# A softmax sum's reciprocal moved from VectorE to ScalarE, and an image's first values loaded by fewer transfers

## Chip, cores and metric

The kernel runs on one core of one Trainium2 chip. The metric is the device time of one execution in microseconds (us); three runs of the kernel before the change give a median of 4012.74 us (4012.72 to 4017.47). Below, PE is TensorE, PEld its weight loads, DVE VectorE, ACT ScalarE, POOL GpSimd, SP the engine whose queue issues nearly all transfers. Each engine works through its own instructions in the program's order and meets the others only at semaphores.

## What is computed

Two residual layers on eight images of 256 channels and 64 x 64 positions, in float32. Cut to what matters:

```
# layer 0: x = x + involution(groupnorm(x))  (1x1 convolutions, a 3x3 weight per position)
# layer 1, on x = groupnorm(x):
q, k, v = 1x1 convolutions of x                     # 4 heads of 64 channels
uk, uv  = 7x7 windows of k + position, v (reflect padding)
out_att = softmax(q . uk) . uv
wts = softmax over 9 taps of (Wfc x)                # 9 weights for each channel and position
oc  = depthwise3x3(relu(depthwise3x3(x, w1)), w2)
out_conv = sum over the 9 taps of oc * wts
x = x + rate1 * out_att + rate2 * out_conv
```

In `out_conv` the same `oc` stands under all nine weights. The kernel takes exponentials relative to one of the taps, sums the other eight (`tot`), adds 1, and multiplies `oc` by the quotient of the sum and itself.

## The kernel before

An image is cut into 8 bands of 8 rows (`R = 8`, `NB = 8`). The program first does layer 0 alone for 12 bands (the loop's `g` from -12 to -1), and then, for 64 bands, layer 1 of band `g` beside layer 0 of a band 10 to 12 places ahead; for the last ten bands no layer 0 is left. Each band of layer 1 has eight steps `s`: two halves of the channels (`ct`), each with four pairs of 8-column tiles (`m`). The order is written out by hand (`manual_schedule`): a step has six places, between which `advance()` is called; work goes in directly, through the lists `mid` and `end` of `beside()`, or by `after(n, f)`, which emits `f` at the n-th `advance()` from there. What is emitted earlier stands earlier in its engine's queue.

In a step, PE does the scores (`sco`, L737), the weighted values (`small <- pt, vt`, L786), two products with `wfc` for the nine weights (`pf`, L873), a transposition (`ptp`, L774), and one or two others: queries, keys (`pk`), values (`pv`, L592), layer 0's maps (L369) and tap weights (`pw`, L466). Most write PSUM tiles of one tag, `gen`, of which there are four; a new one waits until the fourth before it has been read. ACT takes the exponentials of `pf` (`ex`, L878) and of the scores (L759), divides the latter by their sum (L768), and copies. DVE does the depthwise taps (`acc`, L830 and L856), layer 0's products (`prod`, L479), the masked maximum of the scores (`nmax`, L751), a small reciprocal (L766), and the keys with their reflected columns (`kb`, L701 and L708), which the next scores need. POOL adds layer 0's products (`xg`, L487) and the exponentials (`ex`, L1080), copies old keys (L668), and finishes the sum.

`dynamic_sum` (L880 to L911) is emitted four places after the last step of each `ct`, so its parts fall into the steps of the next half band. POOL adds the two halves (L886) and one (L889); 9 and 13 places later DVE takes the reciprocal of half of `tot` each (`quotient`, L894) into `rec`, of which there is one buffer, and POOL multiplies (L895); after 15 places POOL weighs `oc` and adds it to the result `xr` (`weigh`, L899, L900). For `ct = 0` the two reciprocals fall into steps 5 and 6 of the same band, for `ct = 1` into steps 1 and 2 of the next. Only for the very last half band DVE does POOL's part.

Values go through DRAM. `values` makes two halves of a band's `pv` and copies them to `vc` (one buffer); `store_values` writes them to a DRAM tile `vd` with reflected columns; `value_tile` reads `vd` into SBUF tiles `vt` (11 buffers), four for a band (`u`), each for two column groups. At an image's first and last band (`j == 0`, `j == NB`) the reflected rows are read by transfers of their own: eight for a tile in place of two. All of these are issued by SP, in order. An image's first two bands of values are made during the last band of the image before (`made = [(b + 1, 0, 4), (b + 1, 1, 6)]`, the last number being the step); `value_tile` for `j == 0` comes at the end of step 7, for `j == 1` in steps 0, 1 and 2 of the new image's first band, whose step 2 is the first to need them.

Of the kernel before, what the change touches and what calls it, by code (L numbers as in the profile page):

```python
# [12 lines left out]
AF = mybir.ActivationFunctionType  # L13
ALU = mybir.AluOpType
# [9 lines left out]
R = 8  # L24
BAND = R * W
NB = H // R
# [21 lines left out]
PAD = KA // 2  # L48
WP = W + 2 * PAD
TQ = 8  # L50
# [3 lines left out]
KW = TQ + 2 * PAD  # L54
NKEY = KW * KW
CHUNK = R * KW
NPROB = 2 * CHUNK
NEG = -1.0e30


AHEAD = NB + 4
# [25 lines left out]
def conv_layers_kernel(ctx: ExitStack, tc: tile.TileContext, ins: dict, out: bass.AP):  # L87
    nc = tc.nc
# [54 lines left out]
    def rstd_(out_, var, eps):  # L143
        nc.vector.tensor_scalar(out_, var, eps, None, ALU.add)
        nc.scalar.activation(out_, out_, AF.Sqrt)
        nc.vector.reciprocal(out_, out_)


# [61 lines left out]
    images = [Image() for b in range(B)]  # L210
# [4 lines left out]
    def after(n, f):  # L215
        later.append((place[0] + n, f))
# [8 lines left out]
    def gn_affine(sts, means, name, done):  # L225


        n = len(sts)
        mv = stat.tile([P, n, 2], F32, name=f"mv_{name}", tag=f"mv{n}")
        for ct, st in enumerate(sts):  # L230
            nc.vector.bn_aggr(mv[:, ct, :], st)
        mean, var = mv[:, :, 0], mv[:, :, 1]
        gm, d, sc, bi = (stat.tile([P, n], F32, name=f"{v}_{name}", tag=f"{v}{n}") for v in ("gm", "d", "sc", "bi"))

        def group_means(v, k):
            pg = ps.tile([P, n], F32, name=f"pg_{name}_{k}", tag="gen", bufs=4)
            nc.tensor.matmul(pg, means, v, start=True, stop=True)
            return pg


        def a1():
            pg = group_means(mean, 0)
            after(2, lambda: a2(pg))

        def a2(pg):
            nc.vector.tensor_copy(gm, pg)
            for ct in range(n):
                c = slice(ct, ct + 1)
                nc.vector.tensor_scalar(d[:, c], pg[:, c], mean[:, c], None, ALU.subtract)
                nc.vector.tensor_scalar(d[:, c], d[:, c], d[:, c], var[:, c], ALU.mult, ALU.add)  # L250
            after(5, a3)

        def a3():
            pg = group_means(d, 1)
            after(2, lambda: a4(pg))

        def a4(pg):
            nc.vector.tensor_scalar(sc, pg, GN_EPS, None, ALU.add)
            after(2, a5)

        def a5():
            nc.scalar.activation(sc, sc, AF.Sqrt)
            after(4, a6)

        def a6():
            nc.vector.reciprocal(sc, sc)
            for ct in range(n):
                c = slice(ct, ct + 1)
                nc.vector.tensor_scalar(bi[:, c], gm[:, c], sc[:, c], -1.0, ALU.mult, ALU.mult)
            done(sc, bi)  # L270

        after(3, a1)
# [334 lines left out]
    def store_values(b, j):  # L607
# [9 lines left out]
        for d in range(1, PAD + 1):  # L617
            for to, c in ((PAD - d, d), (PAD + W - 1 + d, W - 1 - d)):
# [3 lines left out]
                else:  # L622
                    for p in range(2):
                        o = vd[at + p : at + p + 2 * count[p] - 1 : 2, to : to + 1].rearrange("u c n -> c u n")
                        nc.sync.dma_start(out=o, in_=vc[p * W + c : p * W + c + 1, : count[p]])

    def value_tile(b, j, u):


        im = images[b]  # L630
        vd = im.vd[j]
        vt = im.vt[j, u] = w1.tile([CHUNK, 2, C], F32, tag="vt", name=f"vt_{b}_{j}_{u}", bufs=11)
        if j == 0:
            runs = [(PAD, PAD, R - PAD)] + [(PAD - d, PAD + d, 1) for d in range(1, PAD + 1)]
        elif j < NB:
            runs = [(0, 0, R)]
        else:
            runs = [(0, 1, PAD)] + [(PAD - 1 + d, PAD - d, 1) for d in range(1, PAD + 1)]
        for to, at, n in runs:
            for g in range(2):  # L640
                c0 = (2 * u + g) * TQ
                nc.sync.dma_start(
                    out=vt[to * KW : (to + n) * KW, g], in_=vd[at : at + n, c0 : c0 + KW]
                )

    def new_keys(i):

# [232 lines left out]
    def dynamic_sum(b, i, ct, ex, oc):  # L880

        tot = w1.tile([P, BAND], F32, tag="tots", name=f"tot_{b}_{i}_{ct}", bufs=1)
        xr = images[b].xr[i]

        engine = nc.vector if (b, i, ct) == (B - 1, NB - 1, NCT - 1) else nc.gpsimd
        engine.tensor_add(tot, ex[:, 1], ex[:, 0])  # L886


        engine.tensor_scalar(tot, tot, 1.0, 1.0e37, ALU.add, ALU.min)  # L889
        rec = w1.tile([P, BAND // 2], F32, tag="rec", name=f"rec_{b}_{i}_{ct}", bufs=1)  # L890

        def quotient(u):
            v = tot[:, u * BAND // 2 : (u + 1) * BAND // 2]
            nc.vector.reciprocal(rec, v)  # L894
            after(1, lambda: engine.tensor_mul(v, v, rec))  # L895

        def weigh():

            engine.tensor_mul(oc, oc, tot)  # L899
            engine.tensor_add(xr[:, ct], xr[:, ct], oc)  # L900
            if ct == NCT - 1:
                after(6, store)

        def store():
            nc.sync.dma_start(
                out=out[b].rearrange("(t p) n -> p t n", p=P)[:, :, i * BAND : (i + 1) * BAND], in_=xr
            )

        after(9, lambda: quotient(0))
        after(13, lambda: quotient(1))  # L910
        after(15, weigh)  # L911


    def beside(g, s):

        b, i = divmod(g, NB)
        bn, inx = divmod(g + 1, NB)
        mid, end = [], []

        early = i in (0, NB - 1)  # L920
        if g >= 0:
            if s == 2 - early:
                mid.append(lambda: queries(b, i, 1))
            if s == 3 - early:
                mid.append(lambda: keys(b, i, 1))
        early = inx in (0, NB - 1)
        if 0 <= g + 1 < B * NB:
            if s == 5 - early:
                mid.append(lambda: position(bn, inx))
            if s == 6 - early:  # L930
                mid.append(lambda: queries(bn, inx, 0))
            if s == 7 - early:
                mid.append(lambda: keys(bn, inx, 0))

        made = [(b, i + 2, 4)] if g >= 0 and i < NB - 1 else []
        if i == NB - 1 and 0 <= b + 1 < B:
            made = [(b + 1, 0, 4), (b + 1, 1, 6)]
        for bb, j, d in made:
            if s in (d, d + 1) and (j < NB or s == d):
                mid.append(lambda bb=bb, j=j, d=d: values(bb, j, s - d))  # L940
            if s == d + 1:
                end.append(lambda bb=bb, j=j: store_values(bb, j))
            if s == 7 and d == 4:
                for u in range(NT // 2):
                    end.append(lambda bb=bb, j=j, u=u: value_tile(bb, j, u))
        if g >= 0 and i == 0 and s in (0, 1, 2):
            for u in {0: (0,), 1: (1,), 2: (2, 3)}[s]:
                end.append(lambda u=u: value_tile(b, 1, u))

        nxt = [(b, i + 2, 0)] if g >= 0 and i + 2 < NB else []  # L950
        if i == NB - 1 and 0 <= b + 1 < B:
            nxt = [(b + 1, 0, 0), (b + 1, 1, 1)]
        for bb, ii, d in nxt:
            if s == d:
                end.append(lambda bb=bb, ii=ii: load_rows(bb, ii))
            if s in (d + 1, d + 2):
                end.append(lambda bb=bb, ii=ii, d=d: normalise(bb, ii, s - d - 1))

        alone = g < 0
        if 0 <= g + AHEAD < B * NB:  # L960
            bq_, iq = divmod(g + AHEAD, NB)
            if alone and s == 0:
                mid.append(lambda: small_maps(bq_, iq, small_tile(f"{bq_}_{iq}"))())
            if s == (2 if alone else 0):
                (mid if alone else end).append(lambda: value_maps(bq_, iq, 0))
            if s == (3 if alone else 1):
                mid.append(lambda: value_maps(bq_, iq, 1))
        if 0 <= g + AHEAD - 1 < B * NB and s == (2 if alone else 1):
            bh, ih = divmod(g + AHEAD - 1, NB)

            def hidden():
                parts = hidden_maps(bh, ih, alone)
                if not alone:
                    convs.extend(parts)

            end.append(hidden)
        if 0 <= g + AHEAD - 2 < B * NB and s in TAPS_AT[g < -1]:
            u = TAPS_AT[g < -1].index(s)
            end.append(
                lambda: tap_weights(*divmod(g + AHEAD - 2, NB), u, g < -1, PRODUCTS_AT[g < -1][u])  # L980
            )
        return mid, end
# [24 lines left out]
    with tc.manual_schedule():  # L1007
# [21 lines left out]
        for g in range(-AHEAD, B * NB):  # L1029
            b, i = divmod(g, NB)  # L1030
            for s in range(STEPS):
                ct, m = divmod(s, NT // 2)
                mid, end = beside(g, s)
                steer(g, s)
                if g >= 0:
# [17 lines left out]
                    tot = exponentials(nm, prob, nmax)  # L1053
# [23 lines left out]
                if g >= 0:  # L1077
# [6 lines left out]
                    if m == NT // 2 - 1:  # L1084
                        oc = depthwise_end(b, i, ct, conv[1])
# [96 lines left out]
```

## Time and profile before

| what | value |
|---|---|
| runs | 4012.74 us median of 3 |
| the profiled execution | 4010.67 us; span 4008.9 us from first to last instruction, granted clock 0.988 |
| PE, DVE, ACT, POOL busy | 3807.0, 3419.8, 2839.5, 3174.8 us |
| layer 0 alone, up to the first scores | 246.3 us |
| DVE reciprocals of the sum (L894) | 256 of 1742 ns, 445.9 us |
| POOL products with them (L895) | 254 of 730 ns, 185.4 us |
| transfers `vt <- vd` issued by SP | 960 |

Busy time is the time in which an engine has an instruction running; matmuls are pipelined, so a PE shown busy can still be short of its peak. A wait is idle time of an engine just before an instruction, put down to the instruction that released it. Timeline rows begin with the start in us from the span's start and the duration; neighbouring equal instructions are merged (x2, x3).

### The profile page before, as it was taken

What the parts mean: (1) busy time and instruction counts of PE and PEld (TensorE: products, weight loads), DVE (VectorE), ACT (ScalarE), POOL (GpSimd) and SP (SyncE); (2) the same over time, 40 slices, a digit from 0 to 9 for tenths busy, and PEclk for the clock granted to TensorE, in tenths of its full rate; (3) what the DMA queues carried; (4) which work ended last, traced back from release to release, by engine and by line L of the source; (5) the groups of instructions that cost most, each with busy time, mean ns of one, the idle gap of its engine ahead of it and who ended that gap; (6) DMA issues with size and microseconds to landing.
All of it is one profiled execution on the core that took longest, in us unless ns stands there. A gap on an engine that the chain in (4) does not pass through costs nothing.

```text
span 4008.9 us, 72420 instructions
## 1 busy us (share of the span) xinstructions
PE 3807.0 (95%) x24620; PEld 2116.9 (53%) x24620; DVE 3419.8 (85%) x7143; ACT 2839.5 (71%) x6779; POOL 3174.8 (79%) x2156
## 2 busy tenths in 40 slices
PE   6879999999999999999999999999999999999998
PEld 3445555555555555555555555555555555555554
DVE  5868988888888988888988888978988889977888
ACT  3457777677676777777777677777777677676776
POOL 4758988788987988878887888978888888965665
PEclk9989999999999999999999999999999999999999
DMA  8864543544444443444443544444443544322220
GB/s 230 201 165 113 134 114 104 136 125 113 127 115 122 124 124 101 125 132 120 124 115 104 138 125 118 110 130 124 118 115 90 129 116 104 85 61 88 71 65 32
DMA packets 493171, 469.42 MB, mean 117 GB/s; under 512 B 68432, under 2 KB 394624, under 8 KB 492544
## 3 DMA queue, kind: packets, MB, share of 16 engines
q1 hardware_dynamic: 489472, 460.23, 43.4%
q10 hardware_dynamic: 3328, 4.55, 0.3%
q8 instruction: 195, 3.19, 0.3%
q14 instruction: 176, 1.44, 0.1%
HBM read 325.64 MB, written 138.99 MB: 116 GB/s over the span
## 4 chain that ended last, share of the span: by engine, by line
PE 27%; POOL 26%; DVE 22%; ACT 10%; issue 7%; DMA 5%; SPq 3%; POOLq 0%; DVEq 0%; ACTq 0%
PE pf L873 13%; POOL xg L487 13%; POOL ex L1080 6%; DVE prod L479 5%; DVE acc L856 5%; DVE rec L894 4%; PE small L786 3%; ACT x L343 3%; PE sco L737 2%; PE ptp L774 2%; ACT ex L878 2%; DVE prob L751 2%; DMA x3q<-x 2%; PE pq L672 2%; DVE acc L830 2%
## 5 line engine op out<-in xcount | busy, mean ns | idle before, releaser
L873 PE MATMUL pf<-yp,c_wfc 128*128 128x512 f32 x4096 | 1917.1, 597 | 6.2 <-ACT ex L878 5.1
L487 POOL TENSOR_TENSOR xg<-xg,prod 128x1024 f32<-128x1024 f32 x549 | 1200.7, 2187 | 177.2 <-DVE prod L479 148.3
L873 PEld LDWEIGHTS pf<-yp,c_wfc 128*128 128x128 f32 x4096 | 744.0, 191 | 730.3 <-issue 647.1
L1080 POOL TENSOR_TENSOR ex<-ex,ex 128x1024 f32<-128x1024 f32 x384 | 907.9, 2364 | 55.9 <-ACT ex L878 51.8
L479 DVE SCALAR_TENSOR_TENSOR prod<-pw,c_par,x3q 128x1040 f32<-128x1040 f32 x576 | 737.9, 1288 | 124.8 <-PE pw L466 56.1
L830 DVE SCALAR_TENSOR_TENSOR acc<-yp,c_chan,acc 128x504 f32<-128x504 f32 (+3 forms) x1104 | 775.0, 702 | 50.7 <-ACT acc L821 30.3
L856 DVE SCALAR_TENSOR_TENSOR acc<-hid,c_chan,acc 128x504 f32<-128x504 f32 (+3 forms) x1024 | 749.8, 732 | 18.1
L878 ACT ACTIVATE ex<-pf 128x512 f32<-128x512 f32 x1024 | 602.1, 588 | 204.2 <-PE pf L873 184.3
L759 ACT ACTIVATE prob<-prob,nmax 128x196 f32<-128x196 f32 x1024 | 459.2, 451 | 217.1 <-DVE nmax L751 216.9
L768 ACT ACTIVATE prob<-prob,tot 128x196 f32<-128x196 f32 x1024 | 413.0, 452 | 235.3 <-DVE tot L766 235.1
L895 POOL TENSOR_TENSOR tot<-tot,rec 128x256 f32<-128x256 f32 x254 | 185.4, 730 | 412.9 <-DVE rec L894 387.9
L894 DVE RECIPROCAL rec<-tot 128x256 f32<-128x256 f32 x256 | 445.9, 1742 | 17.2 <-POOL tot L889 12.3
L776 ACT COPY pt<-ptp 112x512 f32<-112x512 f32 x511 | 294.8, 577 | 123.4 <-PE ptp L774 122.3
L751 DVE CUSTOM_DVE_ANT_0 prob<-sco,c_mask 128x196 f32<-128x196 f32 x1024 | 324.5, 354 | 20.4 <-PE sco L737 20.2
L786 PE MATMUL small<-pt,vt 112*64 112x64 f32 x8144 | 300.3, 226 | 37.5 <-DMA vt<-vd 37.1
L774 PEld LDWEIGHTS ptp<-ident,prob 128*112 128x112 f32 x2044 | 228.1, 134 | 188.9 <-issue 135.2
L774 PE MATMUL ptp<-ident,prob 128*112 128x128 f32 x2044 | 322.9, 281 | 1.3 <-ACT vc L600 1.3
L786 PEld LDWEIGHTS small<-pt,vt 112*64 112x64 f32 x8144 | 261.5, 138 | 116.7 <-issue 75.4
L737 PE MATMUL sco<-kb,qb 64*64 64x196 f32 x4096 | 236.1, 343 | 39.6 <-DVE kb L708 32.9
L592 PE MATMUL pv<-c_wv,yp 128*128 128x256 f32 (+1 forms) x1056 | 252.8, 382 | 2.6 <-ACT ex L878 2.1
L369 PE MATMUL p<-xc,w3s 128*128 128x512 f32 x512 | 248.4, 609 | 7.0 <-ACT ex L878 7.0
L466 PEld LDWEIGHTS pw<-h2n,c_c 128*128 128x128 f32 x1152 | 173.3, 191 | 153.5 <-issue 113.1
(139 smaller groups left out, 4756.9 us busy)
## 6 DMA issues: line engine op xcount, KB each, us to landing
vt<-vd SPq DMA_DIRECT2D x448, 112.0 KB
x<-x3n SPq DMA_DIRECT2D x128, 264.0 KB
x3q<-x SPq DMA_DIRECT2D x128, 264.0 KB
xc<-in_x SPq DMA_DIRECT2D x64, 512.0 KB
xg<-in_x SPq DMA_DIRECT2D x256, 128.0 KB
x<-xg SPq DMA_DIRECT2D x256, 128.0 KB
yp<-x SPq DMA_DIRECT2D x128, 256.0 KB
xr<-x SPq DMA_DIRECT2D x64, 512.0 KB
```

The lines of the kernel that those rows point to most:

```text
L479: nc.vector.scalar_tensor_tensor(prod[:, :, :RUN], pw[:, j, :RUN].unsqueeze(1).to_broadcast([P, SHARE, RUN]), par[:, PCB2 + k : PCB2 + k + 1],
L487: nc.gpsimd.tensor_add(im.xg[i], im.xg[i], rows(prod))
L759: nc.scalar.activation(prob[:, h, :NKEY], prob[:, h, :NKEY], AF.Exp, bias=nmax[:, h : h + 1], scale=-1.0, accum_out=tot[:, h : h + 1],)
L768: nc.scalar.activation(prob[:, h, :NKEY], prob[:, h, :NKEY], AF.Copy, scale=tot[:, h : h + 1])
L774: nc.tensor.transpose(ptp[:, h, ch], prob[:, h, ch * CHUNK : (ch + 1) * CHUNK], ident)
L786: nc.tensor.matmul(po[half[h], :, t * TQ : (t + 1) * TQ], im.vt[i + ch, m][:n, t, (2 * ct + h) * HD : (2 * ct + h + 1) * HD], pt[:n, h, ch ...
L830: nc.vector.scalar_tensor_tensor(o, yp[:, ct, ra + dr : rb + dr, ca + dc : cb + dc], chan[:, ct, CW1 + k : CW1 + k + 1], o, ALU.mult, ALU.add,
L856: nc.vector.scalar_tensor_tensor(o, hid[:, ra + dr : rb + dr, ca + dc : cb + dc], chan[:, ct, CW2 + k : CW2 + k + 1], o, ALU.mult, ALU.add,)
L873: nc.tensor.matmul(pf, wfc[:, kt, 2 * m + j, ct * P : (ct + 1) * P], images[b].yp[i][:, kt, PAD : PAD + R], start=(kt == 0), stop=(kt == N ...
L878: nc.scalar.activation(ex[:, j].rearrange("p (r c) -> p r c", r=R), pf, AF.Exp)
L894: nc.vector.reciprocal(rec, v)
L1080: after(4, lambda ex=ex, exb=exb: nc.gpsimd.tensor_add(ex, ex, exb))
```

## The change

It has three parts. The sum's reciprocal: the two DVE reciprocals and two POOL products of a half band become, for each half of `tot`, a logarithm and an exponential of its negative on ACT (into `rec`), and two places later a Newton step of two DVE instructions, which turn `v = tot` into `tot * rec` and then into `(v - 2) * v`, that is the negative of the quotient; `weigh` therefore subtracts, and comes at place 17 instead of 15. The upper bound of the sum is lowered so that its logarithm stays in range, and the ACT table set that holds both functions is loaded by name after each square root. An image's first values: they are made one step sooner, and `value_tile` for its second band is emitted in the middle of steps 0 and 2. Reflected rows: `mirror_rows` copies three rows inside `vd`, DRAM to DRAM, two steps after the values' second step, so that `value_tile` reads a tile with two transfers everywhere.

```diff
+SUM_MAX = 9.0e18
+TABLES = "natural_log_exp_and_others"
...
         nc.scalar.activation(out_, out_, AF.Sqrt)
+        nc.scalar.preload_act_table_set(TABLES)
...
             nc.scalar.activation(sc, sc, AF.Sqrt)
+            nc.scalar.preload_act_table_set(TABLES)
...
+    def mirror_rows(b, j):
+        vd = images[b].vd[j]
+        for d in range(1, PAD + 1):
+            to, at = (PAD - d, PAD + d) if j == 0 else (PAD + d, PAD - d)
+            nc.sync.dma_start(out=vd[to], in_=vd[at])
...
-        if j == 0:
-            runs = [(PAD, PAD, R - PAD)] + [(PAD - d, PAD + d, 1) for d in range(1, PAD + 1)]
-        elif j < NB:
-            runs = [(0, 0, R)]
-        else:
-            runs = [(0, 1, PAD)] + [(PAD - 1 + d, PAD - d, 1) for d in range(1, PAD + 1)]
-        for to, at, n in runs:
-            for g in range(2):
-                c0 = (2 * u + g) * TQ
-                nc.sync.dma_start(
-                    out=vt[to * KW : (to + n) * KW, g], in_=vd[at : at + n, c0 : c0 + KW]
-                )
+        at, n = (0, R) if j < NB else (1, 2 * PAD)
+        for g in range(2):
+            c0 = (2 * u + g) * TQ
+            nc.sync.dma_start(out=vt[: n * KW, g], in_=vd[at : at + n, c0 : c0 + KW])
...
-        engine.tensor_scalar(tot, tot, 1.0, 1.0e37, ALU.add, ALU.min)
+        engine.tensor_scalar(tot, tot, 1.0, SUM_MAX, ALU.add, ALU.min)
...
-            nc.vector.reciprocal(rec, v)
-            after(1, lambda: engine.tensor_mul(v, v, rec))
+            nc.scalar.activation(rec, v, AF.Ln)
+            nc.scalar.activation(rec, rec, AF.Exp, scale=-1.0)
+            after(2, lambda: refine(v))
+
+        def refine(v):
+            nc.vector.scalar_tensor_tensor(v, v, 1.0, rec, ALU.mult, ALU.mult)
+            nc.vector.scalar_tensor_tensor(v, v, 2.0, v, ALU.subtract, ALU.mult)
...
-            engine.tensor_add(xr[:, ct], xr[:, ct], oc)
+            engine.tensor_sub(xr[:, ct], xr[:, ct], oc)
...
-        after(15, weigh)
+        after(17, weigh)
...
-            made = [(b + 1, 0, 4), (b + 1, 1, 6)]
+            made = [(b + 1, 0, 3), (b + 1, 1, 5)]
...
+            if s == d + 2 and j in (0, NB):
+                end.append(lambda bb=bb, j=j: mirror_rows(bb, j))
-            if s == 7 and d == 4:
+            if s == 7 and j != 1:
...
-        if g >= 0 and i == 0 and s in (0, 1, 2):
-            for u in {0: (0,), 1: (1,), 2: (2, 3)}[s]:
-                end.append(lambda u=u: value_tile(b, 1, u))
+        if g >= 0 and i == 0 and s in (0, 2):
+            for u in (s, s + 1):
+                mid.append(lambda u=u: value_tile(b, 1, u))
```

## The prediction

> **What bounds the kernel now.** I read the busy table first, then busy time by stretches, then the waits, and last the timeline of one ordinary band. In the stretches below the columns are span, busy time of PE, PEld, DVE, ACT and POOL (with instruction counts), clock, DMA share and GB/s; the second is most of one band (it runs from 2003.00 to 2061.70), the third lies in the last image, where layer 0 has ended.
>
> ```profile
> PE 3807.0 (95%) x24620; PEld 2116.9 (53%) x24620; DVE 3419.8 (85%) x7143; ACT 2839.5 (71%) x6779; POOL 3174.8 (79%) x2156
> ```
> ```profile
> 2015.50:2061.50 46.00, 44.98 (x295) 25.43 (x294) 43.62 (x86) 32.79 (x78) 41.40 (x27) 1.00 0.47 118
> ```
> ```profile
> 3800.00:3900.00 100.00, 100.00 (x643) 54.50 (x642) 80.06 (x186) 72.73 (x180) 61.64 (x43) 1.00 0.23 70
> ```
>
> PE sets the pace: without layer 0 it never idles. With it, PE loses little, but DVE is busy 43.62 of 46 us and POOL 41.40 (90%): DVE runs level with PE from step 1 to the band's end, and what it gains or loses there soon reaches PE. PE's own waits (total us, times, longest):
>
> ```profile
> PE small L786 <- DMA vt<-vd: 37.1, 15, 8.0
> ...
> PE sco L737 <- DVE kb L708: 32.9, 58, 1.3
> ```
>
> The first is an image's first band waiting for values; the second is the scores of steps 0 and 4 waiting for DVE's keys. Nothing else is as large, so a gain is worth some 70 us at most, plus a little.
>
> **The values.** At an image's start SP issues 32 small `vt` transfers before it gets to the second band's:
>
> ```profile
> 1695.41 16.97 SPq L642 DMA_DIRECT2D vt<-vd  x32
> ...
> 1718.38 1.42 SPq L642 DMA_DIRECT2D vt<-vd  x2
> ```
>
> With two for a tile it is 8 of 16.97/32 = 0.53 us, 4.2 us; 24 go, 12.7 us, and three row copies (estimated at the same 0.5 us each on SP) go in two steps earlier. The second band's store now stands ahead of them, and its first four loads follow, so they land some 10 us sooner, against a longest wait of 8.0: -37.1 us, bounds -37.1 and 0. The same number of transfers goes for each image's last band. Against this: the values' copies into the single `vc` wait for the store of the first band, 14 issues in 1682.36 to 1691.9. Now the second copy follows the first after one step that is not longer than before, with layer 0's sums and queries around it, and ACT can stand there for up to 4.5 us (my estimate from the store's 9.5 us plus some 1.5 to land, less a step of 6.5), with `ex` queued behind it, for which PE waits once its four PSUM tiles are full. I put 0 to 20 us on this over seven images, and take 10.
>
> **The reciprocal, engine by engine.** DVE loses 256 x 1742 ns = 446 us, POOL 254 x 730 = 185 us. ACT gains 512 instructions of 128x256. The nearest row is a scaled copy of just that size, 495 ns: 253 us, 4 us a band, which ACT's idle time (29%) holds. DVE gains 512 products of 128x256, nearest the two that it does itself at the program's very end:
>
> ```profile
> L297 ACT ACTIVATE w3s<-c_w,sc_a 128x256 f32<-128x256 f32 x16 | 7.9, 495 | 0.0
> ...
> L895 DVE TENSOR_TENSOR tot<-tot,rec 128x256 f32<-128x256 f32 x2 | 0.8, 425 | 0.1
> ```
>
> With 0.04 us between dependent ones that is 0.47 each, 241 us: DVE's work falls by 205 us, 3.3 us a band. Two things can take it back, a wait for ACT and a wait for POOL.
>
> *The wait for ACT.* The band's first half, from DVE's timeline:
>
> ```profile
> 2017.01 1.75 DVE L894 RECIPROCAL rec<-tot 128x256 f32<-128x256 f32 x1
> 2018.67 1.21 DVE L479 SCALAR_TENSOR_TENSOR prod<-pw,c_par,x3q 128x1040 f32<-128x1040 f32 x1
> ...
> 2020.87 1.29 DVE L479 SCALAR_TENSOR_TENSOR prod<-pw,c_par,x3q 128x1040 f32<-128x1040 f32 x1
> ...
> 2023.60 1.73 DVE L894 RECIPROCAL rec<-tot 128x256 f32<-128x256 f32 x1
> ...
> 2026.60 1.30 DVE L479 SCALAR_TENSOR_TENSOR prod<-pw,c_par,x3q 128x1040 f32<-128x1040 f32 x1
> ...
> 2031.09 0.73 DVE L701 SCALAR_TENSOR_TENSOR kb<-pk,c_chan,pe 128x512 f32<-128x512 f32 x1
> ```
>
> Without the first reciprocal `prod` is ready to go at 2017.01, but its `pw` matmuls start at 2017.47 (a `prod` that had waited for `pw` began 0.72 us after these), so it goes at 2018.19; then `nmax` and the two additions of L805, which wait for PE at 2020.02, and the first Newton pair stands at 2020.59, ends at 2021.53; `prod` is 0.66 late. Then two taps, and the small reciprocal L766 at 24.18; two taps to 25.61. The second pair follows there, but its exponential is behind L768 on ACT (0.19 after L766: 24.37), the queries' copy (25.09), the logarithm (25.66, 0.53 with its gap) and its own 0.50: done at 26.69. DVE stands for 1.1 us with `prod`, `nmax` and the keys queued behind; the pair ends at 27.69, and `prod` is late by 1.09 against 26.60, and so the keys, the scores behind them on PE, and all of PE. The same sum for the band's second half gives 0.97 (`nmax` at 2058.09 in place of 2057.12). So even with nothing else in the way a half band is 1.0 us later, not sooner: the 1.66 us that each reciprocal took are spent on waiting.
>
> *The wait for POOL.* In this kernel DVE hardly ever takes both inputs of an instruction from SBUF: taps, products and keys have one in PSUM. The Newton products have two in SBUF. The one place before where DVE did that while POOL added is this (from L487's durations, least/median/most, the chain, and the timeline):
>
> ```profile
> L487 POOL TENSOR_TENSOR xg<-xg,prod x549: 2155/2183/4244, 55.5 to 3489.3; 128x1024 f32<-128x1024 f32 x183
> ```
> ```profile
> 60.28 4.24 POOL xg L487
> ```
> ```profile
> 60.19 2.28 DVE L200 TENSOR_TENSOR c_wfc<-c_wfc,last 128x2048 f32<-128x2048 f32 x1
> ```
>
> Of 549 additions one took 4.24 us instead of 2.18, by 2.06 us, the rest of DVE's 2.28: the two did not overlap. There DVE was first. No row shows POOL first, so the cost to DVE is bounded from 0 (DVE is never held) to the rest of POOL's instruction before each product. I take that they exclude each other both ways, as the row is nearest to that. Then, in the first half: POOL's `xg` runs 19.47 to 21.67, the pair starts 1.08 late; the second meets the addition of `ex` (26.10 to 28.46, 2.36 us), 0.64 after its own exponential, and between its two products POOL's copy of the keys can slip in (0.53): `prod` at 29.92, 3.3 us late. In the second half the pairs meet `xg`, the position sum (1.04), `ex` and the keys' copy: `nmax` 3.3 us late again. If the pair is not parted it is 2.8 both times. I take 3.0.
>
> The rule for this is in the Trainium skill, "SBUF — State Buffer", section "Who interferes with whom": an instruction of VectorE with two SBUF inputs and a GpSimd instruction that reads SBUF exclude each other for the whole instruction, whichever starts first. It speaks against the change, and goes further than the row, which shows one direction; by it the full 3.3 us hold.
>
> **The sum.** Layer 0 runs beside bands 0 to 53, 108 half bands. In an image's first and last band the keys of `ct = 1`, and in its last two those for the next band, are emitted a step earlier, ahead of the second pair: 13 and 12 half bands drop out, 83 are left, 83 x 3.0 = 249 us. After band 53 PE is alone at its limit and DVE and POOL have room (80.06 and 61.64 of 100 us): nothing. Values -37 + 10. The last half band's sum, 4 DVE instructions of 2.17 us together a half, becomes about as long: nothing. Eight more table loads of 1.28 us, mostly in the stretch of layer 0 alone, lie beside DVE's products there: nothing, 10 us if not covered. The sum is +222 us on a span of 4008.9. The profiled run took 4010.67, and the median is 2.1 above it: 4012.7 + 222 = 4235 us.
>
> **Rivals.** (1) DVE is not held by POOL, and the exponential still comes late: 83 x 1.0 - 27 = +56, 4069 us. For it: no row shows DVE held. Against: the row above. (2) Faster: DVE is not held, and ACT is ahead of my walk by the 1.1 us, since it loses much time waiting for a slower DVE (L768 for L766: 235.1 us). Then each half band is some 1 us sooner, most of the 32.9 us go (I take 28), and the values' 27: 4012.7 - 55 = 3958 us. It decides where the second exponential is ready by 25.6 in the walk. Against: the chain L766, L768, copy, logarithm, exponential has no gap to shorten but ACT's order. (3) Every pair is parted by a POOL instruction and the 25 half bands left out pay too: 108 x 3.3 - 27 = +329, 4342 us. (4) The parts cancel, 4013: it needs 0.3 us a half band.
>
> **Chances and range.** The forecast's kind, POOL holding DVE, 0.52; (1) 0.18; (3) 0.04; (2) 0.23; (4) 0.03. Runs of this kernel can tell 0.2%, 8 us, from no change: faster 0.23, same 0.03, slower 0.74. The range leaves out the better half of (2) and most of (3): 3960 to 4325. The likeliest case alone spans 2.8 to 3.3 us and 83 to 108 half bands less the values: 4180 to 4325.
>
> **What the new profile would show.** Right: products of L903 and L904 (after) well over 0.47 us in the mean, or DVE idle before them put down to POOL; single POOL additions stretched by some 0.4 us; PE's wait for `kb` grown from 32.9 to over 150 us; PE's wait for `vt` gone. Wrong: L903 and L904 at 0.4 to 0.5 us beside POOL at full speed, and PE's wait for `kb` near zero; then (2). If these products are short but DVE waits for `rec`, (1). If `vt` still shows 20 us or more, the values' part fails; if ACT's wait of `vc` for its store grows beyond 16.5 us (its total before), the 10 us were too few.

## The result, and the profile after

The changed kernel takes 4300.5 us (median of 5 runs, 4297.17 to 4304.95) against 4012.74 us (5 runs, 4010.49 to 4017.47): 1.0713 times, 95% interval 1.0697 to 1.0729, or 287.8 us slower. The forecast was 222 us slower, 4235 us in a range of 3960 to 4325. The profiled execution has a span of 4295.3 us, 286.4 above the one before.

The busy table of the changed kernel's page, and then its groups of instructions (busy us, mean ns of one, idle time before them and its releaser):

```profile
PE 3894.5 (91%) x24620; PEld 2137.1 (50%) x24620; DVE 3471.5 (81%) x7397; ACT 3021.4 (70%) x7299; POOL 3022.7 (70%) x1902
```
```profile
L903 DVE SCALAR_TENSOR_TENSOR tot<-tot,rec 128x256 f32<-128x256 f32 x256 | 263.4, 1029 | 75.2 <-ACT rec L898 73.9 <-POOL ex L1091 0.5
L904 DVE SCALAR_TENSOR_TENSOR tot<-tot 128x256 f32<-128x256 f32 x256 | 202.7, 792 | 8.8
```

DVE was to lose 446 us of reciprocals and gain 241 us of products. The products took 466 us, 1029 and 792 ns each where the row of before had 425, and DVE stood another 74 us for `rec`. A held instruction counts as busy, so DVE's busy time rose by 52 us in all; yet PE (95%), DVE (85%) and POOL (79%) all have a smaller share of the span than before, so the added time is waiting. PE's waits, in the same columns as before (total us, times, longest):

```profile
PE sco L740 <- DVE kb L711: 99.4, 67, 2.9
...
PE pf L876 <- ACT ex L881: 67.3, 44, 3.9
...
PE ptp L777 <- ACT prob L771: 56.0, 35, 4.4
```
```profile
ACT prob L771 <- DVE tot L769: 486.9, 307, 7.9
```

The wait for the keys has tripled from 32.9 us, and two waits for ACT have come up, which in turn waits for DVE: ACT's wait for the small reciprocal (last row) was 235.1 us before. The wait for `vt` (37.1 us before) is no longer in this list. The timeline of one band shows what holds DVE: the first half's pairs, a first product of the second half, and then POOL over the same time.

```profile
2177.53 1.38 DVE L903 SCALAR_TENSOR_TENSOR tot<-tot,rec 128x256 f32<-128x256 f32 x1
2178.95 0.42 DVE L904 SCALAR_TENSOR_TENSOR tot<-tot 128x256 f32<-128x256 f32 x1
...
2184.30 1.22 DVE L903 SCALAR_TENSOR_TENSOR tot<-tot,rec 128x256 f32<-128x256 f32 x1 [0.70 <-ACT rec L898]
2185.55 0.64 DVE L904 SCALAR_TENSOR_TENSOR tot<-tot 128x256 f32<-128x256 f32 x1
...
2211.43 6.47 DVE L903 SCALAR_TENSOR_TENSOR tot<-tot,rec 128x256 f32<-128x256 f32 x1
```
```profile
2176.45 2.18 POOL L491 TENSOR_TENSOR xg<-xg,prod 128x1024 f32<-128x1024 f32 x1 [5.96 <-DVE prod L483]
...
2182.87 2.37 POOL L1091 TENSOR_TENSOR ex<-ex,ex 128x1024 f32<-128x1024 f32 x1
2185.17 0.74 POOL L671 COPY kb<-kb 128x420 f32<-128x420 f32 x1
...
2209.54 2.17 POOL L491 TENSOR_TENSOR xg<-xg,prod 128x1024 f32<-128x1024 f32 x1
2211.68 1.03 POOL L659 TENSOR_TENSOR pe<-pecol,perow 128x512 f32<-128x512 f32 x1
2212.68 2.16 POOL L491 TENSOR_TENSOR xg<-xg,prod 128x1024 f32<-128x1024 f32 x1
2214.81 2.33 POOL L1091 TENSOR_TENSOR ex<-ex,ex 128x1024 f32<-128x1024 f32 x1
2217.09 0.52 POOL L671 COPY kb<-kb 128x420 f32<-128x420 f32 x1
```

The first product begins at 2177.53 while POOL adds until 2178.63; it ends at 2178.91, 0.28 us after POOL, in place of 0.42 us after its own start. The second pair waits for its exponential, then for POOL's addition of `ex`, and its second product is held by the copy of the keys that slipped in. The product at 2211.43 is held through five POOL instructions, 6.47 us. Over the whole execution 283 of the 512 products take more than 0.5 us; what they take above 0.424 us, the longest in e3 below, where none is held, is 248.8 us in all. Each of them began while a POOL instruction ran and ends 0.27 to 0.29 us after the end of a POOL instruction. The products need nothing of these POOL instructions, so the engines do not meet at semaphores alone.

### The profile page after: what moved, and what is told of

The parts are those of the page before. It is cut to its first block, busy times and chain, and to the rows that moved or that the text cites. A ratio compares the mean times of both kernels' runs of the same rounds, so it can differ in the third digit from the quotient of the medians.

```text
span 4295.3 us, 72316 instructions
## 1 busy us (share of the span) xinstructions
PE 3894.5 (91%) x24620; PEld 2137.1 (50%) x24620; DVE 3471.5 (81%) x7397; ACT 3021.4 (70%) x7299; POOL 3022.7 (70%) x1902
## 4 chain that ended last, share of the span: by engine, by line
DVE 36%; PE 33%; ACT 14%; POOL 8%; issue 4%; DMA 2%; SPq 2%; POOLq 0%; ACTq 0%; DVEq 0%
PE pf L876 14%; DVE prod L483 8%; DVE acc L859 7%; DVE tot L903 5%; POOL xg L491 5%; PE small L789 4%; DVE tot L904 4%; PE sco L740 3%; ACT x L347 3%; ACT prob L771 3%; DVE acc L833 2%; PE pv L596 2%; DVE prob L754 2%; PE ptp L777 2%; ACT ex L881 2%
## 5 line engine op out<-in xcount | busy, mean ns | idle before, releaser
L777 PE MATMUL ptp<-ident,prob 128*112 128x128 f32 x2044 | 332.7, 284 | 62.6 <-ACT prob L771 56.0
L740 PE MATMUL sco<-kb,qb 64*64 64x196 f32 x4096 | 243.6, 352 | 106.7 <-DVE kb L711 99.4
L908 POOL TENSOR_TENSOR oc<-oc,tot 128x512 f32<-128x512 f32 x127 | 161.9, 1275 | 244.9 <-DVE tot L904 228.0
L903 DVE SCALAR_TENSOR_TENSOR tot<-tot,rec 128x256 f32<-128x256 f32 x256 | 263.4, 1029 | 75.2 <-ACT rec L898 73.9
L789 PEld LDWEIGHTS small<-pt,vt 112*64 112x64 f32 x8144 | 272.3, 144 | 80.5 <-issue 79.3
L789 PE MATMUL small<-pt,vt 112*64 112x64 f32 x8144 | 309.2, 232 | 0.4
L696 PE MATMUL pk<-yp,c_wk 128*128 128x512 f32 (+2 forms) x576 | 258.8, 578 | 14.5 <-ACT ex L881 6.2
L675 PE MATMUL pq<-yp,c_wq 128*128 128x512 f32 x512 | 242.1, 595 | 21.3 <-ACT ex L881 21.2
```

The lines of the kernel that those rows point to most:

```text
L777: nc.tensor.transpose(ptp[:, h, ch], prob[:, h, ch * CHUNK : (ch + 1) * CHUNK], ident)
L789: nc.tensor.matmul(po[half[h], :, t * TQ : (t + 1) * TQ], im.vt[i + ch, m][:n, t, (2 * ct + h) * HD : (2 * ct + h + 1) * HD], pt[:n, h, ch ...
L903: nc.vector.scalar_tensor_tensor(v, v, 1.0, rec, ALU.mult, ALU.mult)
```

## The experiments

Every kernel was timed in alternation with the kernel before, whose medians lay between 4012.7 and 4015.4 us. Ratios are to it, with 95% intervals.

**e1: the values' part alone.** The kernel before with the diff's hunks for `mirror_rows`, `value_tile` and `made`, and nothing of the reciprocal.

> The kernel before with the values' and the row copies' part of the change alone; the reciprocal stays on DVE. The prediction's theory: PE's wait for vt (37.1 us before) goes, and some 10 us come back through ACT waiting for the store of vc: about 3986 us (3975 to 3995). Rival, the values' part brings nothing (the wait only moves to the values' copies on ACT): 4005 to 4020 us.

Measured 3959.75 us, ratio 0.9867 (0.985 to 0.9883): 53.5 us faster, twice what was expected. PE's and ACT's waits there:

```profile
PE small L785 <- DMA vt<-vd: 2.3, 2, 1.2
...
ACT vc L600 <- DMA vd<-vc: 24.0, 6, 7.4
```

The wait for `vt` falls from 37.1 to 2.3 us. ACT's wait for the store of `vc` grows from 16.5 to 24.0, but PE hardly feels it: an image's last band, where it stands, is 63.5 us long as before. All of the gain lies in the images' first bands, which sum to 53.8 us less; the last bands, whose transfers became fewer too, gain nothing. The fourth image's first band before and in e1 (columns as in the stretches of before; the number after POOL's is the granted clock):

```profile
1699.54:1766.70 67.16, 61.16 (x384) 33.44 (x383) 54.70 (x120) 44.95 (x110) 47.27 (x33) 0.97 0.49 130
1678.64:1739.65 61.01, 59.26 (x383) 32.40 (x383) 54.49 (x120) 44.55 (x108) 47.20 (x33) 1.00 0.57 153
```

PE's idle time falls from 6.00 to 1.75 us, and its busy time falls as well, from 61.16 to 59.26 us, for the same matmuls at a higher clock. Over the eight first bands PE's busy time falls by 18.6 us (484.3 to 465.7), which with the 34.8 us of the wait accounts for the 53.5. Two stretches of the kernel before, the first just after a wait for `vt`, the second a little earlier in the same band:

```profile
1721.30:1726.90 5.60, 4.26 (x20) 2.56 (x21) 3.10 (x5) 2.40 (x4) 1.32 (x1) 0.70 0.89 281
1710.00:1717.00 7.00, 6.23 (x23) 2.99 (x25) 3.61 (x6) 5.93 (x14) 1.32 (x4) 1.00 0.43 111
```

After waits of 2.83 and 1.30 us the granted clock falls to a mean of 0.70 over the next matmuls. The trace has this clock at 1 or at 0.5 of full speed, in stretches of 3.41 us or multiples of it. After the first scores PE works 33.3 us at half clock in the kernel before and 3.4 in this one. So a wait of PE costs more than its length.

**e2: the reciprocal's part alone.** The changed kernel with `made`, `value_tile` and the rows' loads as before.

> The changed kernel with the values and the row copies as before; the reciprocal's part alone. If the values' part is worth -27 us as predicted and the parts add up, the reciprocal's part costs +315 us, more than the 249 that the prediction put on it: about 4327 us (4315 to 4340), and PE's wait for vt is back at some 35 us. Rival, the values' part is worth nothing in the changed kernel: 4295 to 4305 us.

Measured 4333.22 us, ratio 1.0799 (1.0783 to 1.0815): 320 us slower than before, as expected, with PE's wait for `vt` back at 28.9 us. The values' part is worth 33 us beside the new reciprocal and 53 alone; neither part explains the other's cost.

**e3: the two instructions with one SBUF input each.** `accs[0]` is the depthwise accumulator in use, a PSUM tile.

```diff
-            nc.vector.scalar_tensor_tensor(v, v, 1.0, rec, ALU.mult, ALU.mult)
-            nc.vector.scalar_tensor_tensor(v, v, 2.0, v, ALU.subtract, ALU.mult)
+            one = accs[0].rearrange("p r c -> p (r c)")[:, : BAND // 2]
+            nc.vector.scalar_tensor_tensor(v, rec, 1.0, one, ALU.mult, ALU.mult)
+            nc.vector.scalar_tensor_tensor(v, v, 2.0, one, ALU.subtract, ALU.mult)
```

> The changed kernel with the two Newton instructions of the same form, size and place, but each with one input in SBUF and the other in PSUM (a depthwise accumulator of the same half band): the first takes rec and the accumulator, the second tot and the accumulator. So the quotient itself is left out and the output is not the reference's. If DVE is held by POOL because both its inputs lie in SBUF, both instructions fall from means of 1029 and 792 ns to 350 to 430, and only the late exponential is left: the prediction's rival (1), about 4070 us (3960 to 4110). If the exclusion is not the cause (the two products cost what they cost, or their place in the queue does), the time stays above 4230 us.

Measured 4031.73 us, ratio 1.0044 (1.003 to 1.0059). The groups on DVE:

```profile
L907 DVE SCALAR_TENSOR_TENSOR tot<-tot,acc 128x256 f32<-128x256 f32 x256 | 107.6, 420 | 8.8
L906 DVE SCALAR_TENSOR_TENSOR tot<-rec,acc 128x256 f32<-128x256 f32 x256 | 106.5, 416 | 79.6 <-ACT rec L901 74.7 <-POOL ex L1094 0.5 <-ACT hid L424 0.5
```

Same engine, form, size and place, and not one is held: 416 and 420 ns (the longest 424), and 268.8 us of the 4300.5 are gone. This is the experiment that separates the two theories, and it puts 269 us on the two SBUF inputs. Those 248.8 us of holding reach the end at 1.08 to one. Part of this is PE's clock after its waits: PE works 114.1 us at half clock after the first scores in the changed kernel and 9.4 here, so some 52 of the 268.8 us are lost in that way (an estimate, half of the difference). The wait for `rec` is untouched at 74.7 us.

**e4: POOL multiplies, no Newton step.**

```diff
-            nc.vector.scalar_tensor_tensor(v, v, 1.0, rec, ALU.mult, ALU.mult)
-            nc.vector.scalar_tensor_tensor(v, v, 2.0, v, ALU.subtract, ALU.mult)
+            engine.tensor_mul(v, v, rec)
...
-            engine.tensor_sub(xr[:, ct], xr[:, ct], oc)
+            engine.tensor_add(xr[:, ct], xr[:, ct], oc)
```

> The changed kernel without the Newton step: POOL multiplies tot by rec, as before the change, two places after the exponential, and weighs with a sum again; DVE does nothing for the quotient. The Newton step is left out. If all of the loss comes from DVE's two instructions (being held and waiting for the exponential), this is faster than before: DVE is 446 us lighter, PE's 32.9 us for kb and 37.1 us for vt go for the most part, 3940 to 3975 us. If ACT's 512 extra instructions or their place cost much by themselves, it is above 4050 us.

Measured 3904.86 us, ratio 0.9726 (0.9712 to 0.9741), better than expected. ACT's 512 extra instructions cost nothing that shows inside the bands. Against e1 it is 54.9 us for 446 us of DVE's reciprocals: PE sets the pace, so most of what DVE is spared is idle time.

**e6: logarithm and exponential one place earlier, with one SBUF input.**

```diff
-            after(2, lambda: refine(v))
+            after(3, lambda: refine(v))
...
-        after(9, lambda: quotient(0))
-        after(13, lambda: quotient(1))
+        after(8, lambda: quotient(0))
+        after(12, lambda: quotient(1))
```

> The kernel whose Newton instructions have one SBUF input each (the quotient left out), with logarithm and exponential emitted one place earlier on ACT (ahead of the probabilities and the queries' copy), DVE's order unchanged. If what is left of the reciprocal's cost there (4031.7 against 3959.8 us of the values' part alone) is DVE standing for the late exponential, DVE's wait for rec (74.7 us) goes and the time falls to 3955 to 3985 us. If it is the 512 instructions' own time on DVE, the wait goes but the time stays at 4020 to 4035 us. If the exponential then stands on ACT for the single rec buffer, with the probabilities behind it, it is slower than 4035 us.

Measured 3984.6 us, ratio 0.9924 (0.991 to 0.9937): 47.1 us less than e3.

```profile
L906 DVE SCALAR_TENSOR_TENSOR tot<-rec,acc 128x256 f32<-128x256 f32 x256 | 106.6, 417 | 19.9 <-ACT acc L856 2.9 <-ACT rec L901 1.4 <-ACT prob L772 0.5
```

The wait for `rec` is 1.4 us. So of the 72.0 us between e1 and e3, 47 were the late exponential. Of the 24.9 that remain, 10.6 lie before the first scores (255.97 against 245.34 us, see e5); the other 14 are not traced.

**e7: the same move in the changed kernel.** The diff of e6, on the products with two SBUF inputs.

> The changed kernel with the same move of logarithm and exponential and nothing else. If the waits add up, it falls by what the move brings beside the one-input instructions, to some 4230 us (4210 to 4260), and the products stay at means near 1.0 and 0.8 us. If a product that comes earlier only stands longer for POOL, the time stays at 4285 to 4305 us and the products' means grow by as much as the wait for rec shrinks.

Measured 4249.48 us, ratio 1.0583 (1.0568 to 1.0597): 51.0 us less than the change, as if the waits added up.

```profile
L903 DVE SCALAR_TENSOR_TENSOR tot<-tot,rec 128x256 f32<-128x256 f32 x256 | 308.8, 1206 | 2.5 <-ACT rec L898 2.5
L904 DVE SCALAR_TENSOR_TENSOR tot<-tot 128x256 f32<-128x256 f32 x256 | 205.4, 802 | 8.8
```

Yet the lines agree with neither theory in full: the wait for `rec` shrinks by 71.4 us and the first products grow by 45.4. A product that comes earlier does stand longer for POOL, and the time falls all the same; why the two effects did not cancel more is not settled.

**e8: only the first product with two SBUF inputs.** The diff of e3 for the second instruction alone.

> The changed kernel in which only the first Newton instruction has both inputs in SBUF (tot and rec, as in the change); the second takes tot and a depthwise accumulator in PSUM, so the second half of the Newton step is left out. If each held instruction passes its hold on to the end one for one, the first one's 256 x (1029 - 416) ns = 157 us go on top of the 4031.7 us with neither: 4180 to 4205 us, the second is back at some 0.41 us. If being held once a pair is what counts (the second is held only because the first let a POOL instruction in), the first one is held longer and the time is above 4260 us.

Measured 4221.07 us, ratio 1.051 (1.0495 to 1.0524), 189 us above e3, and just above the 4180 to 4205 expected of a hold that is passed on.

```profile
L906 DVE SCALAR_TENSOR_TENSOR tot<-tot,rec 128x256 f32<-128x256 f32 x256 | 273.3, 1067 | 75.4 <-ACT rec L901 73.6 <-POOL ex L1094 0.5
L907 DVE SCALAR_TENSOR_TENSOR tot<-tot,acc 128x256 f32<-128x256 f32 x256 | 107.7, 421 | 8.8
```

The first one is held 164.6 us in all and costs 189, 1.15 to one. The second, behind it in the same queue, is not held at all.

**e11: one POOL instruction an image moved away.** Every image has one product like the one at 2211.43 (six in the execution, 36.2 us). Each began 0.26 to 0.29 us before the end of POOL's addition, and POOL's next instruction followed without a pause. The products that got their turn after one instruction began at least 0.33 us before its end, or, six of them, 0.16 to 0.19 us before it with POOL idle for over 2 us behind.

```diff
-                nc.gpsimd.memset(d[:, :, 0], 0.0)
+                nc.vector.memset(d[:, :, 0], 0.0)
```

> The changed kernel with one small POOL instruction an image moved to DVE: the memset of the first row of x3q (0.53 us, L395), which in the band before an image's last two but one shifts POOL so that a first Newton product begins 0.26 to 0.29 us before the end of POOL's addition and is then held 6.0 us, through five POOL instructions (six times in the execution; every other held product there got its turn after one). If that start close to the end is what loses the turn, the six long holds fall to about 1 us, that band from 69.3 to some 63 to 65 us, and the time to 4260 to 4276 us. If the row of ready POOL instructions behind the addition is what keeps DVE out, the six holds stay and the time is 4293 to 4305 us.

Measured 4288.17 us, ratio 1.0676 (1.0658 to 1.0693), between the two.

```profile
L903 DVE SCALAR_TENSOR_TENSOR tot<-tot,rec 128x256 f32<-128x256 f32 x256 | 231.6, 905 | 75.1 <-ACT rec L898 74.2
L904 DVE SCALAR_TENSOR_TENSOR tot<-tot 128x256 f32<-128x256 f32 x256 | 214.1, 836 | 8.8
```

The long holds are gone: none lasts through more than one instruction, and that band falls from 69.3 to about 66 us. But the second products take up 11.4 us of the 31.8 that the first ones lose, and the stretch before the first scores is 2.7 us longer. That a start near POOL's end loses the turn fits this, but is not enough by itself: in e8 seven products that began as near to it (0.25 to 0.27 us) were let in after one instruction. Behind these POOL had nothing to run for 0.8 us. Nor is a ready POOL instruction enough, for products that began 0.33 us or more before the end got in ahead of one. All 24 long holds of the changed kernel, e2, e7 and e8 have both, a start 0.25 to 0.29 us before the end and a POOL instruction directly behind. Why that start loses the turn stays open.

**e9: the Newton step on POOL.**

```diff
-            nc.vector.scalar_tensor_tensor(v, v, 1.0, rec, ALU.mult, ALU.mult)
-            nc.vector.scalar_tensor_tensor(v, v, 2.0, v, ALU.subtract, ALU.mult)
+            engine.tensor_mul(v, v, rec)
+            engine.tensor_scalar(rec, v, 2.0, None, ALU.subtract)
+            engine.tensor_mul(v, v, rec)
```

> The changed kernel with the whole Newton step on POOL: a product, a subtraction and a second product for each half of tot, in the place of DVE's two instructions; all the table loads as in the change. No DVE instruction has two SBUF inputs beside POOL. POOL carries two instructions more than in the kernel with POOL's product alone, by the rows 0.73 us (128x256 product) and, as half of the 1.92 us of the 128x512 form, 0.96 us: 1.7 us twice in a half band, 435 us in all. In that kernel POOL is busy 39.8 of 46 us inside a band; with 6.8 us more in a band of 57.4 us it would be full. If POOL then sets the pace, 3960 to 4060 us; if its idle time holds the step, 3905 to 3930 us. In both cases far below 4300, since nothing is held.

Measured 4195.32 us, ratio 1.0447 (1.0433 to 1.0461). The expectation failed: nothing is held, and 290 us are lost against e4. ACT's waits:

```profile
ACT ex L881 <- POOL ex L1092: 292.0, 143, 4.4
...
ACT rec L897 <- POOL tot L905: 115.8, 54, 2.9
```

POOL falls behind, and ACT waits for it to free the buffers of `ex` (three) and `rec` (one); PE in turn waits 122.9 us for ACT's `ex`. The expectation had 1 to 3 us a band for a full POOL; most bands grew by 5 to 6 us (1, 2, 4 and 5 of the fourth image from 57.4 to between 62.5 and 63.6), as the late engine stops a third one.

**e5: e4 with fewer table loads before the first scores.**

```diff
-        nc.scalar.preload_act_table_set(TABLES)
...
-            nc.scalar.preload_act_table_set(TABLES)
+            if name not in ("a0", "a1"):
+                nc.scalar.preload_act_table_set(TABLES)
```

> The kernel with POOL's product and no Newton step, and in addition without the named table loads after the square roots of the two small weight norms and of the first two images' first norm, where layer 0 runs alone; the later ones stay. The stretch before the first scores was 253.7 us with them against 245.3 us in the kernel with the values' part alone. If the extra table loads are not covered there, that stretch comes back to some 246 us and the time to about 3897 us (3893 to 3901). If they are covered and the longer stretch has another cause, 3902 to 3908 us.

Measured 3899.85 us, ratio 0.9715 (0.9702 to 0.9729): 5.0 us less than e4, and the stretch before the first scores falls from 253.7 to 247.4. Most of the extra 8 us there were table loads. This is the fastest version of the study, 112.9 us below the kernel before it and 400.7 below the change. A stretch of it beside layer 0, in the columns of the stretches shown of before:

```profile
2015.00:2061.00 46.00, 45.81 (x304) 26.12 (x302) 37.49 (x89) 37.00 (x91) 39.77 (x29) 1.00 0.44 115
```

PE is busy 45.81 of 46 us, where it was 44.98; DVE has fallen from 43.62 to 37.49.

**e10: e5 with the exponential one place earlier.** The diff of e6, on e5.

> The fastest kernel so far (POOL's product, no Newton step, fewer table loads: 3899.9 us) with logarithm and exponential one place earlier. There PE is busy 45.8 of 46 us inside a band. If PE is the bound, an earlier exponential brings nothing: 3896 to 3904 us. If POOL's 165 us of waiting for rec still reaches PE, 3880 to 3893 us.

Measured 3947.77 us, ratio 0.9833 (0.982 to 0.9847): 47.9 us slower than e5, which neither theory had.

```profile
ACT rec L897 <- POOL tot L903: 147.4, 54, 3.6
```

The second logarithm overwrites the one `rec` buffer, so it waits for POOL's product of the first half (33.9 us of such waits in e5); and since it now stands ahead of the probabilities in ACT's queue, these wait too (PE then waits 20.1 us for them, where it had no such wait in e5). In e6 the reader of `rec` was DVE, which is prompt, and the same move gained 47.1 us.

Durations of one image's bands (the fourth; from the first scores of a band to those of the next, us), and the time by which products are held in the changed kernel:

| band | before | e1 | e4 | e3 | changed | held |
|---|---|---|---|---|---|---|
| 0 | 67.16 | 61.02 | 60.29 | 63.08 | 67.78 | 3.63 |
| 1 | 58.36 | 58.38 | 57.37 | 59.84 | 65.95 | 4.63 |
| 2 | 58.39 | 58.37 | 57.41 | 59.68 | 66.17 | 4.91 |
| 3 | 60.60 | 60.61 | 59.19 | 61.08 | 65.46 | 4.33 |
| 4 | 58.95 | 58.94 | 57.37 | 59.67 | 63.30 | 3.56 |
| 5 | 58.69 | 58.69 | 57.34 | 59.69 | 69.27 | 8.02 |
| 6 | 56.60 | 56.57 | 55.85 | 57.56 | 61.19 | 3.81 |
| 7 | 63.47 | 63.54 | 62.15 | 64.96 | 66.52 | 3.60 |

## Why the prediction was right, and where its sum was short

**The kind was right.** The change is slower because DVE is held by POOL at two instructions with two SBUF inputs, with a late exponential beside it. The row it rested on showed only DVE first; the runs show POOL first, 283 times. The Trainium skill, "SBUF — State Buffer", section "Who interferes with whom", says that the two exclude each other for the whole instruction, whoever is first, and that an instruction with at most one SBUF input does not contend. The runs agree with both: each held product ends 0.27 to 0.29 us after a POOL instruction, 1029 and 792 ns in the mean with two inputs, against 416 and 420 ns with one (e3).

**Term by term.** The prediction's sum was -27 us for the values and 83 half bands of 3.0 us, of which 1.0 (83 us) was the late exponential and 2.0 (166 us) the holding. The runs give -53.5 us (e1), +72.0 us (e3 less e1) and +268.8 us (changed less e3), together 287.3. That these add up shows nothing, as they are three steps on one way from the kernel before to the changed one; beside the new reciprocal the values are worth 33 us (e2), not 53.5.

- *The wait for ACT* was put at 83 us, and the step measured 72.0, but in part by luck: only 47.1 of it go when the exponential comes earlier (e6). Another 10.4 lie before the first scores, where the prediction had put the table loads at nothing, and some 14 are not traced.
- *The holding* was mis-sized, 166 against 268.8 us, though the size of one ordinary hold was right: without the six long ones the 102 other half bands beside layer 0 are held for 2.0 us each (206 us). The difference between e3 and the change, summed over bands 0 to 53 of the traces (270.4 us), shows three places. In bands 0, 6 and 7 of the images, where 25 half bands were dropped "out" because their keys are emitted earlier, it is 62.6 us and not 26. The table shows 3.6 to 3.8 us held there, hardly less than elsewhere; keys emitted early do not help when `prod`, `nmax` and the taps behind the pair are late as well, and only band 7 absorbs most of it (1.56 us longer). In band 5 it is 63.7 us and not 28: the walk had POOL slipping one copy in between the two products, and no product losing its turn again and again. In bands 1 to 4 it is 144.2 us and not 112, with some 121 us held: a hold costs more than its length there, in part by PE's half clock.
- *The values* brought 53.5 us alone, where -37.1 was set as the bound of the gain. The wait itself was right (37.1 to 2.3 us); the step that failed took a wait of PE for its length, and left out the slower clock after it. The same is missing from the holding: PE works 114.1 us at half clock in the changed kernel, against 33.3 before. The cap on any gain, "some 70 us", was the sum of two such waits and fell with them: e5 gains 112.9.
- *The 10 us for the single `vc`* were not there: ACT's wait grew as the estimate said, but the last bands by only 0.1 us each. In the changed kernel it is 10.9 us.
- *The table loads* were put at nothing beside layer 0 alone, or 10 us if not covered. They were not covered: some 6 of 8 us in e4 (see e5). In the changed kernel the stretch before the first scores is 3.7 us longer than before (250.06 against 246.34 us).

**The rivals.** (1), DVE not held and a late exponential, is what e3 builds: 4031.7 against the 4069 worked out, and the 37 us between are the values (26.5) and the smaller wait (11). (2), faster, is e6, with the exponential early and nothing held: 3984.6 against 3958; its condition, an exponential ready in time, was rightly doubted, as DVE waited for `rec` 111 times. (3), all 108 half bands paying, was nearest in the size, 4342 us, though its reason, a pair parted every time, was not: 148 of the 256 second products are not held. The span given for the likeliest case, 4180 to 4325, does not come out of its terms: 83 times 2.8 and 108 times 3.3, less 27, give 4218 to 4342 us. The measured time lies in both.

**Signs that missed.** PE's wait for `kb` was to pass 150 us and came to 99.4: the lateness reaches PE at two other places as well, `ex` and the probabilities. POOL's stretched additions were to show some 0.4 us; the addition or position sum that follows a held product is longer by 0.16 to 0.20 us (1.23 against 1.04 for the position sum).

## What to carry over

Before elementwise work with two SBUF operands is moved onto VectorE, look at what GpSimd does at that time: the price is the rest of GpSimd's instruction, each time. Here it passed to the end at 1.08 to one where VectorE is level with PE, and hardly at all where it is not: in the last ten bands, without layer 0, 6.9 us are held and the time of those bands grows by 0.1 us against e3. An operand in PSUM (e3, which leaves the quotient out) or the product left with GpSimd (e4) took the hold away, 269 and 396 us less than the change, where an earlier exponential brought 51 (e7). And moving an instruction earlier in a queue is a gain only if its buffer is free: ask who read the buffer last (e6 gained 47 us and e10 lost 48 by the same move).

## What the hardware showed unasked

A held VectorE instruction usually gets its turn after one GpSimd instruction, but in six places an execution it waited through five back to back, 6.0 us. How little GpSimd has to go hardly changes the end: six products that began with 0.16 to 0.19 us of its instruction left also ended 0.28 us after it and took 0.44 to 0.47 us. Only in e8, with 0.12 to 0.13 us left, did seven take the usual 0.43.

PE's granted clock falls after a wait. In the changed kernel, after PE stood 4.37 us for the probabilities:

```profile
2220.60:2227.60 7.00, 6.98 (x12) 2.98 (x12) 6.19 (x18) 5.22 (x14) 4.28 (x3) 0.57 0.33 103
...
2158.30:2162.40 4.10, 3.96 (x54) 3.14 (x56) 2.06 (x6) 1.69 (x4) 3.94 (x3) 0.58 0.69 229
```

PE is busy nearly all of both stretches, at 0.57 and 0.58 of its clock. The second follows a wait of 2.93 us. The Trainium skill, "TensorE: Matmul & The Clock Gate", section "What's actually happening", gives about 3.4 us of idling before the clock halves; here waits of 2.93 us, and of 2.83 and 1.30 us close together, were followed by it, so less than that was enough.
